# A two-layer graph transformer on one core: four buffers of gathered keys and values, an MLP in halves, and roots by a power

## The chip, the cores and the metric

The kernel runs on one core of one Trainium2 chip. The metric is the device time of one execution in microseconds. A core has a tensor engine (PE, with its weight loads listed apart as PEld), a vector engine (DVE), a scalar engine (ACT), GpSimd (POOL) and a sync engine (SP), each with its own queue of instructions, taken in order. DMA transfers are issued from SP, ACT and POOL; a gather or scatter by indices (DMA_INDIRECT) is issued from POOL.

## What is computed

3125 nodes of 256 features, 50000 edges, two layers. Layer 0 is a graph sum, a linear attention with MLP, and a dense mixture of eight experts. Layer 1, in which the change lies, adds an edge attention (`_L1_gnn_ref`), a "hyperbolic" branch (`_L1_mix_ref`) and a routed mixture of experts (`_L1_ffn_ref`, the two best of eight, plus a shared MLP). Shortened:

```python
# edge attention
q, k, v = feat @ Wq.T + bq, feat @ Wk.T + bk, feat @ Wv.T + bv          # 8 heads of 32
score = clip(einsum('ehd,ehd->eh', q[edge_dst], k[edge_src]) / sqrt(HD), -10, 10)
alpha = softmax of score over the edges of each edge_dst
wv = segment_sum(alpha * v[edge_src], edge_dst)
x = feat + wv @ Wp.T + bp
h = layernorm(x) * ln_g + ln_b
gnn = x + gelu(h @ W1.T + b1) @ W2.T + b2                                # 256 -> 1024 -> 256
# hyperbolic branch: norms, and a division by a norm, several times
n = clip(norm(u), 1e-15); tanh(n) * u / n; arctanh(min(n, 1 - 1e-5)) * p / n
# x = x + gnn + mix; then x = x + shared MLP + the two routed experts
```

Both branches take many reciprocal square roots of small vectors: one number a node for the layer norms and for the norms.

## The kernel before

*Tiles.* The nodes are 25 tiles of 125; `CHUNKS` are seven groups of four tiles (the last has one). The edges are sorted by target node; each node tile has a list of 17 x 128 edge slots, in three groups of 6, 6 and 5 (`GRP`): 75 groups in all.

*An order written by a planner.* Each stage is written as generators ("streams") that yield `Op(engine, cost, after, take, give)` before they issue instructions. `Flow.run` (L126) keeps a time for every engine and for every buffer, and at each step resumes the stream whose operation can start first; ties go to the lower urgency, the first argument of `flow.add`. `take` and `give` count buffers (`Flow(kvg=3, ...)`, L1478). When an operation is done its users may start after its end, its `lag`, and `HOP = 0.2` (L91, L143). The costs are figures in the code, in us; they decide the order of the instructions in each engine's queue and nothing else. The chip runs that order with semaphores.

*Layer 0* is recorded by a Flow of its own; its MLP uses the same `mlp_stream` (L636) with the name "m". *Layer 1* (`layer1`, L1443) is one Flow with these streams:

- `group` (L1498), one for each of the 75 groups: POOL gathers the keys and values of its 6 x 128 edges from `kvtab` into a buffer `kvg` (one DMA_INDIRECT for 128 edges, L1504); SP loads the tile's queries `q3`, the transposed one-hot matrix `ST` and the one-hot matrix `Sb`; PE spreads the queries over the edges (`qe`, L1540); DVE multiplies them into the keys (L1544), sums over a head (`sco`, L1563) and clips (L1568); ACT takes the exponential (L1570); DVE multiplies it into the values (L1573); PE sums the edges of each node (`es`, L1581), which gives the buffer `kvg` back.
- `attend` (L1585), one a tile: the division by the sum, a transpose `wvT`, the matmul `wp`.
- `mlp_stream` with the name "g", one a chunk of up to four tiles: layer norm on DVE with `rsqrt`, two transposes into PSUM, ACT's scaling into `hT`, eight pairs of matmuls `hp_g` (L683; 500 columns), a GELU each into one of eight buffers `hid` (L675), then the second product `dn_g` tile by tile (L697).
- `hyper` (L1612), one a tile, in pairs of tiles: SP loads `z`, ACT applies six ReLUs (L1625), PE transposes and multiplies into `cat` (L1642, L1644), a root `nn` a pair; then reciprocals and products on DVE, a transpose `oT` and the matmul `ft`. `hyper_end` (L1714), one a chunk: roots `n3` and `n4`.
- Then `route_in` (layer norm and logits), `routing`, `scatter`, and the experts: `shared` (L1968, matmuls `hp_s` and `dn_s`), `fetched` and `routed` (32 tiles of 256 rows, `rh` L2059 and `ry` L2074), `finish`, `collect`.

*A root* (`rsqrt`, L287) is a bit-level first guess by two integer operations and three Newton steps of three operations: eleven DVE instructions on a tile of one to four columns.

GELU and the exponential need different function tables on ACT; the compiler puts an ACT_TABLE_LOAD wherever the queue goes from one to the other.

Of the kernel before, what the change touches and what calls it, by code (L numbers as in the profile page):

```python
# [18 lines left out]
C = 256  # L19
E = 50000  # L20
P = 125
# [65 lines left out]
class Flow:  # L87
# [3 lines left out]
    HOP = 0.2  # L91
    TABLE = 1.28

    def __init__(self, **buffers):
        self.free = {}
        self.buffers = {tag: [0.0] * n for tag, n in buffers.items()}
        self.streams = []
        self.table = None
# [27 lines left out]
    def run(self):  # L126
        live = [s for s in sorted(self.streams, key=lambda s: s[:2]) if self._resume(s, None)]
        while live:
            best, at_ = None, None
            for s in live:  # L130
                t = self._start(s[3])
                if t is not None and (best is None or t < at_ - 1e-6):
                    best, at_ = s, t
            assert best is not None, "streams that wait for each other"
            op = best[3]
            for tag in op.take:
                self.buffers[tag].remove(min(self.buffers[tag]))
            end = at_ + op.cost
            self.free[op.eng] = end
            if op.table is not None:  # L140
                self.table = op.table
            done = Mark()
            done.time = end + op.lag + self.HOP  # L143
            for tag in op.give:
                self.buffers[tag].append(done.time)
            if not self._resume(best, done):
                live.remove(best)
# [3 lines left out]
def kernel(ctx: ExitStack, tc: tile.TileContext, a: dict, out: bass.AP):  # L151
# [71 lines left out]
    def row(pool, name, parts=P):  # L223
# [43 lines left out]
                   allow_small_or_imprecise_dtypes=True)  # L267
    tiny = keep.tile([128, 1], F32, name="tiny")
# [18 lines left out]
    def rsqrt(v, n, name, parts=P):  # L287

        y = small.tile([parts, n], F32, tag=f"rsy{n}", name=f"rsy_{name}", bufs=6)
        g = small.tile([parts, n], F32, tag=f"rsg{n}", name=f"rsg_{name}", bufs=6)  # L290
# [7 lines left out]
        return y  # L298

# [336 lines left out]
    def mlp_stream(c, inputs, name, pool_of, w1, w2, g, b, b1, done, start=None):  # L636

        t0, nt = CHUNKS[c]
        n = nt * P
        mv = small.tile([P, 4, 2], F32, tag=f"mv_{name}", name=f"mv_{name}{c}", bufs=2)  # L640
        for j in range(nt):
            m = yield Op("DVE", 0.6, [inputs[t0 + j]])
            st = small.tile([P, 6], F32, tag="st", name=f"st_{name}{c}_{j}")
            nc.vector.bn_stats(st, XN[c][:, j, :])
            nc.vector.bn_aggr(mv[:, j, :], st)
            m2 = yield Op("DVE", 0.42, [m])
            nc.vector.tensor_tensor(X[c][:, j, :], X[c][:, j, :], XN[c][:, j, :], OP.add)
        m = yield Op("DVE", 2.1, [m])
        var = small.tile([P, 4], F32, tag="rs", name=f"var_{name}{c}")
        nc.vector.tensor_scalar(var[:, :nt], mv[:, :nt, 1], 1e-5, None, op0=OP.add)  # L650
        rs = rsqrt(var[:, :nt], nt, f"{name}{c}")
        for j in range(nt):
            m = yield Op("DVE", 0.36, [m, m2])
            nc.vector.tensor_scalar(XN[c][:, j, :], XN[c][:, j, :], mv[:, j, 0:1],
# [3 lines left out]
        pt = [mm_tile([128, 512], f"tr_{name}_{c}_{k}") for k in range(2)]  # L658
        for k in range(2):
            for j in range(nt):  # L660
                nc.tensor.transpose(pt[k][:, j * P : (j + 1) * P],
                                    XN[c][:, j, k * 128 : (k + 1) * 128], ident[:P, :P])
        for k in range(2):
            m = yield Op("ACT", 0.56, [mk], take=["hT"] if k == 0 else [], give=["mm"])
            if k == 0:
                hT = pool_of().tile([128, 2, 4 * P], F32, tag="hT", name=f"hT_{name}_{c}")
# [3 lines left out]
        def gelu():  # L670
# [3 lines left out]
            hm = pool_of().tile([128, 4 * P], F32, tag="hid", name=f"hid_{name}{c}_{q}", bufs=8)  # L674
# [3 lines left out]
        for h in range(8):  # L678
            mk = yield Op("PE", 0.0035 * n, [m], take=["mm", "hid"],
                          give=["hT", "mlp"] if h == 7 else [])  # L680
            ps = mm_tile([128, 512], f"hp_{name}{c}_{h}")
# [6 lines left out]
        for j in range(nt):  # L688
            for q in range(0, 8, 4):
# [4 lines left out]
                if q == 0:  # L694
                    po = nm_tile([P, C], f"dn_{name}{c}_{j}")
# [4 lines left out]
            nc.vector.tensor_tensor(X[c][:, j, :], po, X[c][:, j, :], OP.add)  # L700
# [742 lines left out]
    def layer1(lists):  # L1443
# [23 lines left out]
        for m in range(6):  # L1467
# [10 lines left out]
        flow = Flow(kvg=3, S=3, Sb=2, ST=2, q3=2, qe=2, ed=1, mm=2, nm=3, z=1, cat=2, r=2,  # L1478
                    oT=1, ft=5, ch=2, sc=1, mlp=1, hT=1, hid=8,
                    mh=8, rhid=8, rw=2, xr=2, xrT=2, yr=2, to=3)  # L1480
        attended_ = [Mark() for _ in range(T)]
        mlp_, hyp_ = [Mark() for _ in CHUNKS], [Mark() for _ in CHUNKS]
# [15 lines left out]
        def group(b, gi, blk):  # L1498
# [3 lines left out]
            kvg = ep.tile([128, 6, 2 * C + NH], F32, tag="kvg", name=f"kvg_{nm}", bufs=3)  # L1502
# [82 lines left out]
        def attend(b, blk):  # L1585
# [15 lines left out]
            wT = ep.tile([128, 2, P], F32, tag="wT", name=f"wvT_{b}", bufs=2)  # L1601
# [10 lines left out]
        def hyper(t, pair, ch):  # L1612
# [6 lines left out]
            if t == t0:  # L1619
# [3 lines left out]
                for i in range(6):  # L1623
                    mk = yield Op("ACT", 0.43, [m])
# [7 lines left out]
            for i in range(4):  # L1632
                s, h = divmod(i, 2)
                last = i == 3 and t == t0 + nt - 1
                mk = yield Op("PE", 0.75 if s == 0 else 1.4, [pair["ready"]],
# [32 lines left out]
            if t == t0 + nt - 1:  # L1668
                m = yield Op("DVE", 2.3, [m, full])
# [3 lines left out]
                y = rsqrt(nn, nt, f"nn{t}")  # L1673
# [22 lines left out]
            m = yield Op("PE", 0.96, [m], take=["mm"], give=["r"])  # L1696
# [17 lines left out]
        def hyper_end(c, ch):  # L1714
            t0, nt = CHUNKS[c]
            m = yield Op("DVE", 2.3, ch["done"])
            n3, s3, n4 = ch["n3"][:, :nt], ch["s3"][:, :nt], ch["n4"][:, :nt]
            nc.vector.tensor_scalar(n3, n3, MIN_NORM ** 2, None, op0=OP.max)
            y = rsqrt(n3, nt, f"n3{c}")
# [12 lines left out]
            m = yield Op("DVE", 2.3, [m])  # L1732
            nc.vector.tensor_scalar(n4, n4, MIN_NORM ** 2, None, op0=OP.max)
            y = rsqrt(n4, nt, f"n4{c}")
# [44 lines left out]
        def after_all():  # L1779
            m = yield Op("SP", 0.5, mlp_ + hyp_)  # L1780
# [4 lines left out]
        def route_in(c):  # L1785
            t0, nt = CHUNKS[c]
            n = nt * P
            m = yield Op("DVE", 0.6 * nt + 2.1, [mlp_[c], hyp_[c], moe_])
# [179 lines left out]
        def shared(c):  # L1968
# [11 lines left out]
            for h in range(8):  # L1980
                tag = ("mm", "qe")[h % 2]
                mk = yield Op("PE", 0.0035 * n, [turned_[c], moe_], take=[tag, "mh"])
# [7 lines left out]
            for j in range(nt):  # L1990
                for q in range(0, 8, 4):
                    if j == 0 and q == 4:
                        yield from gelu()
                    m = yield Op("PE", 1.75, [acts[q + 3]], take=["nm"] if q == 0 else [],
                                 give=["mh"] * 8 if j == nt - 1 and q == 4 else [])
# [123 lines left out]
        for c, (t0, nt) in enumerate(CHUNKS):  # L2119
            flow.add(t0 + 8, mlp_stream(c, attended_, "g", lambda: lp, w1, w2, "gnn_g", "gnn_b", "gnn_b1",  # L2120
                                   mlp_[c], big_))
# [197 lines left out]
```

## Time and profile before

| | us |
|---|---|
| median of 3 runs | 2899.23 (2895.84 to 2901.83) |
| the profiled execution | 2883.45, its span 2881.6 |
| PE busy (instructions) | 2537.6, 88% (11409) |
| PE weight loads | 1836.7, 64% |
| DVE | 1390.3, 48% (3497) |
| ACT | 968.3, 34% (2001) |
| POOL | 1149.4, 40% (1145) |
| mean granted clock of PE | 0.946 |

Times in the profile are microseconds, unless they stand as ns. A line of the costliest groups reads: line of the kernel, engine, operation, output<-inputs, shapes, count | busy us, mean ns of one | idle us of the engine just before them, and what ended most of it. A line of waits reads: who waited at which line <- for whom: us in all, times, the longest. The page's row of slices gives the busy share in 40 equal parts of the span (72 us each) in tenths. Layer 0 fills about the first 18 slices, the attention of layer 1 the next eleven or so (the first gather of `kvg` starts at 1308.81 us), routing and experts the rest.

### The profile page before, as it was taken

The page shows a single profiled execution, that of the slowest core. Times are in us where ns is not written, and L with a number is a line of the kernel's source. Part 1 is how long each engine was busy: PE and PEld are TensorE (multiplying, and loading weights), DVE is VectorE, ACT ScalarE, POOL GpSimd, SP SyncE. Part 2 cuts the span into 40 slices and gives each one's busy share as a digit, 9 for nine tenths or more (in the row PEclk, how much of TensorE's full clock was granted, in tenths as well). Part 3 has the DMA queues.
Part 4 walks back from the last instruction along what each step waited for, and adds up shares of the span by engine and source line. Part 5 has one row for each costly group of instructions (what it writes and reads, how often), then busy time and mean ns, then how long its engine had stood idle before and what let it go on. Part 6 is the DMA issues. An engine that isn't in the chain of part 4 may idle for free. (4 is left out here: it accounts for less than half of the span.)

```text
span 2881.6 us, 32246 instructions
## 1 busy us (share of the span) xinstructions
PE 2537.6 (88%) x11409; PEld 1836.7 (64%) x11409; DVE 1390.3 (48%) x3497; ACT 968.3 (34%) x2001; POOL 1149.4 (40%) x1145
## 2 busy tenths in 40 slices
PE   3889988888998999996677888878888999999998
PEld 2556665655665555564556666666666668888886
DVE  5365123252443242456778798878798301111113
ACT  3673111122222343344334454434433212222221
POOL 3002667766673010004555554545441452222220
PEclk8979999999999999997889999999999999999999
DMA  4425555565562004317666665556550145555554
GB/s 106 134 95 174 153 172 169 158 182 162 158 197 84 25 26 125 82 37 243 187 183 201 189 192 171 173 170 185 166 156 17 41 142 189 196 192 192 192 174 139
DMA packets 186999, 427.01 MB, mean 148 GB/s; under 512 B 31434, under 2 KB 116554, under 8 KB 178635
## 3 DMA queue, kind: packets, MB, share of 16 engines
q0 software_dynamic: 80688, 281.78, 32.5%
q1 hardware_dynamic: 103593, 140.99, 15.7%
q10 hardware_dynamic: 2545, 2.09, 0.3%
q8 instruction: 92, 1.51, 0.2%
q14 instruction: 81, 0.66, 0.1%
HBM read 358.95 MB, written 65.74 MB: 147 GB/s over the span
## 5 line engine op out<-in xcount | busy, mean ns | idle before, releaser
L1504 POOL DMA_INDIRECT kvg<-kvtab,el x425 | 453.4, 1067 | 372.3 <-issue 111.3
L1063 POOL DMA_INDIRECT msg<-hs,el x425 | 421.9, 993 | 407.9 <-DMA hot<-S 209.6
L1175 ACT ACTIVATE fh<-fp,bnh,bns 128x500 f32<-128x500 f32 (+1 forms) x224 | 159.7, 723 | 411.1 <-PE fp L1171 288.9
L1581 PE MATMUL es<-kvg,S 128*125 128x264 f32 x850 | 231.9, 427 | 53.3 <-DVE kvg L1573 48.1
L1540 PE MATMUL qe<-q,ST 125*128 125x256 bf16 x1275 | 176.8, 280 | 74.2 <-DVE kvg L1544 53.9
L1186 DVE SCALAR_TENSOR_TENSOR x<-fy,f_w,x 125x256 f32<-125x256 f32 x200 | 95.8, 482 | 300.7 <-PE fy L1183 192.4
L2059 PE MATMUL rh<-xrT,rw 128*128 128x256 f32 x1024 | 237.3, 380 | 0.0
L1581 PEld LDWEIGHTS es<-kvg,S 128*125 128x125 f32 x850 | 170.5, 206 | 102.8 <-DVE kvg L1573 59.6
L1183 PE MATMUL fy<-f_Wo,fh 128*125 128x256 f32 x800 | 210.4, 386 | 29.1 <-DVE x L1186 18.6
L2047 ACT ACTIVATE rhid<-rh,rw 128x256 f32<-128x256 f32 x256 | 121.5, 475 | 337.1 <-PE rh L2059 312.8
L2074 PE MATMUL ry<-rw,rhid 128*128 128x256 f32 x1024 | 231.5, 379 | 0.0
L1092 PEld LDWEIGHTS <-S 128*125 128x125 bf16 x1275 | 158.8, 143 | 90.9 <-issue 72.4
L2074 PEld LDWEIGHTS ry<-rw,rhid 128*128 128x128 f32 x1024 | 194.6, 190 | 26.9 <-issue 0.5
L1092 PE MATMUL es<-msg,S 128*125 128x256 bf16 x1275 | 188.2, 284 | 22.3 <-DMA msg<-hs,el 13.0
L2059 PEld LDWEIGHTS rh<-xrT,rw 128*128 128x128 f32 x1024 | 189.4, 190 | 28.6 <-ACT rhid L2047 5.0
L2081 DVE TENSOR_TENSOR yr<-ry,rw 128x256 f32<-128x256 f32 x64 | 27.2, 425 | 357.6 <-PE ry L2074 357.6
L1540 PEld LDWEIGHTS <-ST 125*128 125x128 bf16 x1275 | 127.3, 100 | 113.6 <-issue 77.7
L1183 PEld LDWEIGHTS fy<-f_Wo,fh 128*125 128x125 f32 x800 | 143.1, 190 | 88.5 <-issue 40.1
L1171 PE MATMUL fp<-fh,f_W 128*128 128x500 f32 (+1 forms) x448 | 187.6, 545 | 4.2 <-ACT fh L1175 3.8
L1171 PE MATMUL fp<-xT_f,f_W 128*128 128x500 f32 (+1 forms) x448 | 188.5, 547 | 0.0
L1544 DVE TENSOR_TENSOR kvg<-qe,kvg 128x512 f32<-128x512 f32 (+1 forms) x225 | 143.1, 652 | 50.2 <-PE qe L1540 22.8
L1299 POOL TENSOR_TENSOR xn<-xn,row_bp 125x1024 f32<-125x1024 f32 (+1 forms) x7 | 13.8, 1974 | 379.4 <-DVE hx L1273 192.5
(422 smaller groups left out, 4242.3 us busy)
## 6 DMA issues: line engine op xcount, KB each, us to landing
db<-dlT SPq DMA_DIRECT2D x25, 544.0 KB
ST<-dlT SPq DMA_DIRECT2D x25, 544.0 KB
hot<-S SPq DMA_DIRECT2D x50, 187.5 KB
Sb<-hot SPq DMA_DIRECT2D x50, 187.5 KB
ztab<-z SPq DMA_DIRECT2D x18, 500.0 KB
z<-ztab SPq DMA_DIRECT2D x12, 750.0 KB
xs<-pad SPq DMA_DIRECT2D x1, 8224.0 KB
xr<-xs SPq DMA_DIRECT2D x32, 257.0 KB
```

Of the source, the lines that this page charges most:

```text
L1063: nc.gpsimd.indirect_dma_start(out=msg[:, i, :], out_offset=None, in_=hs3_rows, in_offset=bass.IndirectOffsetOnAxis(ap=el[:, b, g0 + i : g ...
L1092: nc.tensor.matmul(blk["po"], S[:, i, :], msg[:, i, r * C : (r + 1) * C], start=(g0 + i == 0 and r == 0), stop=(g0 + i == LE - 1 and r == 2))
L1171: nc.tensor.matmul(ps[q][:, :n], self.ws[e][i][:, k, q * 128 : (q + 1) * 128], h[:, k, :n], start=(k == 0), stop=(k == 1))
L1175: nc.scalar.activation(nxt[:, q, :n], ps[q][:, :n], AF.Relu, bias=self.sh[i][:, 2 * e + q : 2 * e + q + 1], scale=self.sc[i][:, 2 * e + q ...
L1183: nc.tensor.matmul(po, nxt[:, k, j * P : (j + 1) * P], self.ws[e][2][:, k, :], start=(k == 0), stop=(k == 1))
L1504: nc.gpsimd.indirect_dma_start(out=kvg[:, i, : 2 * C], out_offset=None, in_=kvtab, in_offset=bass.IndirectOffsetOnAxis(ap=el[:, b, g0 + i ...
L1540: nc.tensor.matmul(pq[i0][:, i, :], ST[:P, g0 + i0 + i, :], blk["q3"][:, r, :], start=(r == 0), stop=(r == 2))
L1544: nc.vector.tensor_tensor(kvg[:, i0 : i0 + k, :C], pq[i0][:, :k, :], kvg[:, i0 : i0 + k, :C], OP.mult)
L1581: nc.tensor.matmul(blk["pa"], S[:, i, :], kvg[:, i, C:], start=(g0 + i == 0), stop=(g0 + i == LE - 1))
L2047: nc.scalar.activation(hid[-1][:, q % 2, :], ps, AF.Gelu, bias=w1[:, 8 * C + q : 8 * C + q + 1])
L2059: nc.tensor.matmul(ps, w1[:, k * 4 * C + h * 128 : k * 4 * C + (h + 1) * 128], xrT[:, k, :], start=(k == 0), stop=(k == 1))
L2074: nc.tensor.matmul(po, hid[k // 2][:, k % 2, r * 128 : (r + 1) * 128], w2[:, k * C : (k + 1) * C], start=(k == 0), stop=(k == 7))
```

## The change

Six edits:

1. `kvg` has four buffers instead of three (in the planner and in the pool).
2. `mlp_stream` takes a part of a chunk: in layer 1 two tiles at a time, thirteen streams instead of seven, with `hT` and `hid` half as wide and the urgency `t0 + h_ + 6` instead of `t0 + 8`. `wT` has one buffer instead of two; the buffers of wide roots go from six to one.
3. Layer 1's planner counts 0.5 us instead of 0.2 from an operation to its users (`hop`).
4. A new `rsqrt_by_power` takes the layer norm's root in the MLP of layer 1 and the roots `nn`, `n3` and `n4`: one power on POOL, then one Newton step of three operations on DVE. The roots in layer 0 and in `route_in` stay.
5. Some of the planner's costs are others: z 0.55 for 0.43, cat 0.48 and 0.86 for 0.75 and 1.4, oT 0.62 for 0.96; the first product of the MLP 0.0039 a column for 0.0035, in both layers.
6. The shared MLP of the experts takes a token `shared`, so that the planner lets one chunk of it run at a time.

```diff
-    HOP = 0.2
-    def __init__(self, **buffers):
+    def __init__(self, hop=0.2, **buffers):
+        self.hop = hop
...
-            done.time = end + op.lag + self.HOP
+            done.time = end + op.lag + self.hop
...
+    minus_half = keep.tile([128, 4], F32, name="minus_half")
+    nc.vector.memset(minus_half, -0.5)
...
+    def rsqrt_by_power(v, n, name, m):
+
+        y = small.tile([P, n], F32, tag=f"rpy{n}", name=f"rpy_{name}", bufs=8)
+        g = small.tile([P, n], F32, tag=f"rpg{n}", name=f"rpg_{name}", bufs=8)
+        m = yield Op("POOL", 0.65, [m])
+        nc.gpsimd.tensor_tensor(y, v, minus_half[:P, :n], OP.pow)
+        m = yield Op("DVE", 0.5, [m])
+        nc.vector.scalar_tensor_tensor(g, y, -0.5, v, op0=OP.mult, op1=OP.mult)
+        nc.vector.tensor_tensor(g, g, y, OP.mult)
+        nc.vector.scalar_tensor_tensor(y, g, 1.5, y, op0=OP.add, op1=OP.mult)
+        return y, m
...
-    def mlp_stream(c, inputs, name, pool_of, w1, w2, g, b, b1, done, start=None):
+    def mlp_stream(c, inputs, name, pool_of, w1, w2, g, b, b1, done, start=None, part_=(0, 4)):
-        t0, nt = CHUNKS[c]
+        j0, cap = part_
+        t0, nt = CHUNKS[c][0] + j0, min(cap, CHUNKS[c][1] - j0)
...
+            m = yield Op("DVE", 0.17, [m])
+            var = small.tile([P, 4], F32, tag="mvar", name=f"var_{name}{t0}", bufs=len(CHUNKS))
+            nc.vector.tensor_scalar(var[:, :nt], mv[:, :nt, 1], 1e-5, None, op0=OP.add)
+            rs, m = yield from rsqrt_by_power(var[:, :nt], nt, f"{name}{t0}", m)
...
-                hT = pool_of().tile([128, 2, 4 * P], F32, tag="hT", name=f"hT_{name}_{c}")
+                hT = pool_of().tile([128, 2, cap * P], F32, tag="hT", name=f"hT_{name}_{t0}")
...
-            hm = pool_of().tile([128, 4 * P], F32, tag="hid", name=f"hid_{name}{c}_{q}", bufs=8)
+            hm = pool_of().tile([128, cap * P], F32, tag="hid", name=f"hid_{name}{t0}_{q}", bufs=8)
...
-        flow = Flow(kvg=3, S=3, Sb=2, ST=2, q3=2, qe=2, ed=1, mm=2, nm=3, z=1, cat=2, r=2,
+        flow = Flow(hop=0.5, kvg=4, S=3, Sb=2, ST=2, q3=2, qe=2, ed=1, mm=2, nm=3, z=1, cat=2, r=2,
...
-            kvg = ep.tile([128, 6, 2 * C + NH], F32, tag="kvg", name=f"kvg_{nm}", bufs=3)
+            kvg = ep.tile([128, 6, 2 * C + NH], F32, tag="kvg", name=f"kvg_{nm}", bufs=4)
...
-            wT = ep.tile([128, 2, P], F32, tag="wT", name=f"wvT_{b}", bufs=2)
+            wT = ep.tile([128, 2, P], F32, tag="wT", name=f"wvT_{b}", bufs=1)
...
-                m = yield Op("DVE", 2.3, [m, full])
+                m = yield Op("DVE", 0.4, [m, full])
...
-                y = rsqrt(nn, nt, f"nn{t}")
+                y, m = yield from rsqrt_by_power(nn, nt, f"nn{t}", m)
+                m = yield Op("DVE", 0.17, [m])
...
-                mk = yield Op("PE", 0.0035 * n, [turned_[c], moe_], take=[tag, "mh"])
+                mk = yield Op("PE", 0.0035 * n, [turned_[c], moe_],
+                              take=[tag, "mh"] + (["shared"] if h == 0 else []))
...
-            flow.add(t0 + 8, mlp_stream(c, attended_, "g", lambda: lp, w1, w2, "gnn_g", "gnn_b", "gnn_b1",
-                                   mlp_[c], big_))
+            for h_ in range(0, nt, 2):
+                flow.add(t0 + h_ + 6, mlp_stream(c, attended_, "g", lambda: lp, w1, w2, "gnn_g", "gnn_b",
+                                            "gnn_b1", mlp_[c][h_ // 2], big_, (h_, 2)))
```

## The prediction

> **What bounds the kernel now.** I began with the page's forty slices: where is the tensor engine (PE) full, and where not?
>
> ```profile
> PE   3889988888998999996677888878888999999998
> DVE  5365123252443242456778798878798301111113
> PEclk8979999999999999997889999999999999999999
> ```
>
> From slice 33 on (2375 us) PE is full and DVE nearly idle: the routed MLP costs what PE costs. In slices 18 to 29 both stand at 6 to 9 and neither is full. That is the attention of the second layer, which the change edits. I cut it out by windows (length, then busy us of PE, weight loads, DVE, ACT, POOL; then granted clock, DMA share, GB/s).
>
> ```profile
> 1308.00:2175.00 867.00, 688.44 (x3567) 528.13 (x3567) 698.31 (x1358) 362.28 (x894) 453.39 (x425) 0.91 0.60 183
> 1308.00:1525.00 217.00, 145.87 (x770) 114.52 (x770) 158.46 (x280) 78.22 (x214) 123.08 (x115) 0.84 0.69 210
> 1525.00:2175.00 650.00, 542.57 (x2799) 413.62 (x2798) 539.85 (x1079) 284.06 (x681) 330.31 (x311) 0.93 0.58 174
> 2350.00:2375.00 25.00, 19.85 (x76) 14.08 (x75) 2.04 (x5) 6.00 (x12) 0.95 (x1) 0.93 0.58 212
> ```
>
> Of 867 us PE is busy 79% and DVE 81%: two queues that wait for each other in turn. The waits of this stage say on what (total us, times, longest):
>
> ```profile
> POOL kvg L1504 <- PE qe L1540: 104.7, 20, 18.3
> PE qe L1540 <- DVE kvg L1544: 53.9, 31, 9.2
> PE es L1581 <- DVE kvg L1573: 48.1, 35, 6.1
> DVE kvg L1573 <- ACT kvg L1570: 12.6, 8, 5.5
> ```
>
> POOL's gathers wait for a buffer to come back; PE waits 102 us for the two products of a group on DVE. The chain of waits in this window gives its largest PE lines (es 7.1%, dn_g 5.2%, hp_g 4.6%, qe 4.0%) 20.9% and its largest DVE lines (4.9, 3.8, 3.5, 2.5%) 14.7%. So where work leaves DVE, I let 14.7/35.6 = 0.41 of it reach the end, and 0.59 where it is added to PE. That is a choice: the bounds are 0 and 1.
>
> **The change, part by part.** Counts and places come from the instruction order of both built programs, durations from the trace of before.
>
> *Roots.* A root is eleven DVE instructions in a row:
>
> ```profile
> 1343.19 0.17 DVE L291 TENSOR_SCALAR rsg_nn<-nn 125x2 int32<-125x2 int32 x1
> 1343.40 0.17 DVE L292 TENSOR_SCALAR rsy_nn<-rsg_nn 125x2 int32<-125x2 int32 x1
> ...
> 1345.36 0.17 DVE L1674 TENSOR_SCALAR s<-rsy_nn 125x2 f32<-125x2 f32 x1
> ```
>
> That is (1345.36 - 1343.19)/11 = 0.197 us each. The 27 roots of the hyperbolic branch (13 + 7 + 7) keep three on DVE: 27 x 8 x 0.197 = 42.6 us. The MLP's go from 7 x 12 instructions (with the epsilon) to 13 x 4: 32 x 0.197 = 6.3 us. DVE loses 49 us; times 0.41: **-20** (bounds 0 and -49).
>
> Each of the 40 roots now goes to POOL and back. The power is not in the trace; its nearest rows are the smallest two-operand operation and a one-column one:
>
> ```profile
> L1299 POOL TENSOR_TENSOR xn<-xn,row_bp 125x256 f32<-125x256 f32 x1 | 0.7, 745 | 27.6 <-PE qe L1540 27.6
> L805 POOL TENSOR_SCALAR pad<-part 128x1 f32<-128x1 f32 x1 | 0.2, 217 | 0.1
> L1504 POOL DMA_INDIRECT kvg<-kvtab,el x425 | 453.4, 1067 | 372.3 <-issue 111.3 <-PE qe L1540 104.7 <-DVE sco L1568 39.7
> ```
>
> 0.22 to 0.75 us; with two to four columns nearer the lower row, but with an operation not shown, so I take 0.6. The queue it joins weighs more. Gathers hold POOL (453.4 + 111.3)/867 = 65% of the stage, in groups of six, 6 x 1.33 = 8 us. DVE is in order: all behind a waiting root waits too, the products of later groups first, and then PE for those. In the new order 24 roots have over 5 us of other DVE work between the question and the use of the answer; that work hides them. Sixteen have 0 to 4.8 us, 1.9 on average. Such a root meets a group with chance 0.65 and waits half of it: 0.65 x 4 + 0.6 - 1.9 = 1.3 us, 16 x 1.3 = 21 us on DVE, x 0.41: **+8** (bounds 0, all at once; and 16 x (8 + 0.75 - 1.9) = 110).
>
> *Fourth buffer and larger distance.* One edit for the clock: a gather may run ahead by one more group, and the order puts more between an operation and its user. Bounds: 0, and the 102 us in which PE waits for the group's products. A buffer now returns every fourth group instead of every third, so a quarter of these waits: **-25**. Below nothing it is possible as well: SP's queue is moved too. In the new order the first q3 and ST loads stand behind the last five ztab stores, and some z loads one or two Sb loads later; z is what six ReLUs and PE's cat matmuls wait for. At 1312.75 the first z load was issued in before; two loads ahead of it cost about **+2** at the start.
>
> *MLP by two tiles.* PE makes 384 passes of 250 columns for 192 of 500 (32 of 125 stay).
>
> ```profile
> L2059 PE MATMUL rh<-xrT,rw 128*128 128x256 f32 x1024 | 237.3, 380 | 0.0
> L1985 PE MATMUL hp_s<-xT_f,pw1s 128*128 128x500 f32 (+1 forms) x224 | 88.8, 547 | 1.0 <-ACT xT_f L1804 1.0
> L675 ACT ACTIVATE hid_g<-hp_g,pv 128x500 f32<-128x500 f32 (+1 forms) x56 | 35.1, 633 | 33.5 <-PE hp_g L683 23.1 <-issue 7.7 <-PE qe L1540 2.4
> L675 ACT ACT_TABLE_LOAD x15 | 19.2, 1283 | 0.3
> ```
>
> At 256 columns a pass takes 237.3/1024 = 0.232 us, so 0.226 at 250; at 500 the passes stand 0.42 apart (weight loads at 2824.10 and 2824.52 in the timeline). 384 x 0.226 - 192 x 0.42 = 6.1 us (0 if exactly half; 19 at the stage's es rate, 231.9/850 x 250/264 = 0.258). Times 0.59: **+4**. ACT gets 104 GELUs of about 0.475 (the row of rhid) for 56 of 0.633, +14, and 26 scalings for 14, +5. It is idle 58% of the stage; that hides both. The tables are another thing: between the first and the last exponential the order holds 29 table loads before and 55 after, since GELU and exponential alternate more finely. A load takes 1.28 us and the next activation begins at once (a load at 1660.38, its exponential at 1661.67). 26 x 1.29 = 34 us more on ACT, 13 of the loads ahead of an exponential, on the path sco, exp, kvg. DVE waits 12.6 us there now for 75 groups. I take 13 x 1.29 = 17, a third of it felt: **+5** (bounds 0 and 34).
>
> The Trainium skill, "ScalarE: Activation LUTs", section "What ACT_TABLE_LOAD costs", speaks against this: a switch costs 1283 ns plus a drain of about 1380. The trace has the first and no second. By the page the 26 would cost 69 us and the sum would be about 5 us worse. "GPSIMD Engine Reference", section 4.1, sends elementwise work on tiles to VectorE; for a tile of four columns behind gathers the rows above decide.
>
> *Elsewhere.* In the first layer the planner books more for the MLP's first product, and its matmuls slide by a few places against the edges' (0, bounds +-5: PE is 85 to 95% busy there). Behind the routing PE idles 5.15 us in 2350 to 2375, until xr is read back; the new order lets three hidden blocks of the shared MLP run there (three times 1.7 us): **-4**.
>
> Sum: -20 + 8 - 25 + 2 + 4 + 5 - 4 = **-30 us**. The profiled execution took 2883.45 (span 2881.6), 16 below the median of the runs, 2899.2; by the median this gives **2869 us**.
>
> **The rivals.** (1) *Eaten up*: all 26 loads felt (+29 on my sum: 2898), or the fourth buffer brings nothing because POOL's waits put down to PE qe are the product's late return, which more distance doesn't shorten (+25: 2894). For it: 104.7 us name a qe matmul, which frees no buffer. Against it: POOL does wait 372.3 - 111.3 = 261 us at this line. (2) *Slower*: the root behind a group of gathers takes the place of the eleven instructions. Sixteen short covers, and a loop: a gather waits for the es matmul of four groups back, the root behind it for the gather, DVE for the root. It decides once all 40 roots cost DVE 94 us (38/0.41), 2.35 each; at 3.5 each: (140 - 94) x 0.41 = +19, 2918 us. Against it: 24 roots have cover. (3) *More*: both engines reach the later part's 83.5% from the start. PE's 694 us at 0.835 make 831 of 867, and DVE's work would allow less; with the -4 behind the routing, 2859 or below.
>
> **How the numbers follow.** Forecast together with (3) 0.58, its own range 2835 to 2890; (1) 0.20, between 2890 and 2905; (2) 0.22. A measurement here can tell about 0.2% (6 us) from no change. Of (1) half is still faster by that, 0.08 within, 0.02 slower: faster 0.68, same 0.08, slower 0.24. The range leaves one in ten on each side: 2826 to 2920.
>
> **What would show it.** Right: DVE's busy time 40 us or more lower, PE's waits L1544 and L1573 together well below 102, the stage from first gather to last es 25 to 35 us shorter, the MoE part the same to 5 us. Wrong: DVE idle before the first instruction after a power, put down to POOL, over 90 us in all; ACT's exponentials waiting for nothing but table loads while DVE waits for them; PE over 19 us busier in hp_g.

## The result, and the profile after

| | us |
|---|---|
| changed kernel, median of 4 runs | 2928.97 (2910.76 to 2937.72) |
| kernel before, median of 4 runs | 2897.53 (2893.91 to 2901.83) |
| ratio, 95% interval | 1.0103, 1.0056 to 1.0150 |
| profiled execution, changed (before) | 2910.76, span 2908.5 (2883.45, span 2881.6) |
| DVE busy | 1347.3 (1390.3) |
| ACT busy | 1013.6 (968.3) |
| POOL busy | 1167.8 (1149.4) |
| mean granted clock of PE | 0.941 (0.946) |

The change made the kernel 31 us slower; 2869 was forecast, and 2826 to 2920 as the range. The 2% verdict calls this the same; the interval does not.

The three rows of the forty slices that opened the prediction, of the changed kernel (72.7 us a slice):

```profile
PE   3888978989899999995788778887788999999998
DVE  5364122253534253354788677777778201111113
PEclk8989999999999999996899889998998999999999
```

DVE's 8s and 9s in slices 23 to 29 became 7s: the roots did leave it. PE did not fill up in exchange.

Where the 27 us between the two spans came in is read from windows cut at four instructions: first gather of `kvg`, first `es`, last `es`, first `hp_s` (the shared MLP), end. Columns: window, length, then busy us of PE, weight loads, DVE, ACT, POOL, then granted clock, DMA share, GB/s. The kernel before:

```profile
1308.80:1342.30 33.50, 16.54 (x90) 13.54 (x89) 11.51 (x27) 16.69 (x46) 16.25 (x17) 0.70 0.73 238
1342.30:2161.10 818.80, 658.12 (x3412) 504.02 (x3413) 676.73 (x1289) 337.92 (x829) 437.14 (x408) 0.92 0.60 183
2161.10:2224.70 63.60, 53.50 (x242) 40.05 (x241) 55.43 (x222) 19.50 (x46) 9.55 (x4) 0.92 0.06 19
2224.70:2881.60 656.90, 643.85 (x2922) 528.02 (x2922) 111.41 (x294) 164.32 (x326) 195.15 (x231) 0.99 0.48 160
```

The changed kernel, cut at the same instructions:

```profile
1312.70:1363.70 51.00, 20.19 (x96) 15.02 (x94) 16.56 (x34) 19.67 (x51) 22.73 (x24) 0.63 0.77 254
1363.70:2180.30 816.60, 659.32 (x3576) 537.56 (x3577) 626.86 (x1050) 377.35 (x890) 449.35 (x435) 0.91 0.58 178
2180.30:2250.10 69.80, 55.57 (x263) 47.38 (x261) 61.51 (x216) 23.12 (x64) 19.89 (x12) 0.85 0.06 18
2250.10:2908.50 658.40, 643.92 (x2922) 531.72 (x2922) 105.32 (x282) 163.58 (x326) 189.94 (x229) 0.99 0.48 159
```

First gather 3.9 us later, 17.5 more to the first `es`, 2.2 less in the middle, 6.2 more in the tail, 1.5 more in the experts: together the 26.9. The loss is at the start; the puzzle is the middle, where DVE has 50 us less to do and only 2 us were won.

The waits of the attention stage of the changed kernel (who waited at which line <- for whom: us, times, longest). L1526 is the gather, L1562 `qe`, L1566 and L1595 the two products, L1603 `es`, L307 the power:

```profile
POOL kvg L1526 <- PE es L1603: 60.4, 12, 13.3
POOL kvg L1526 <- PE qe L1562: 58.6, 15, 12.3
PE qe L1562 <- DVE kvg L1566: 57.7, 26, 7.9
DVE kvg L1566 <- remote: 49.2, 13, 16.3
POOL rpy_nn L307 <- DVE nn L1694: 42.2, 4, 19.4
POOL rpy_g L307 <- DVE var_g L671: 34.5, 5, 16.6
POOL rpy_n L307 <- DVE n L1741: 28.7, 4, 12.6
ACT wvT L1624 <- remote: 24.3, 4, 6.9
...
PE es L1603 <- DVE kvg L1595: 20.1, 12, 5.7
```

PE's waits for the two products fell from 102.0 to 77.8, as far as this trace names them (how far, the experiments tell). Two kinds of wait have grown. POOL stands 105 us at a power, for an operand of DVE, in 13 times; for 48 us of them gathers still stand behind in its queue, 57 lie after the last gather. And DVE and ACT wait for "remote": the view finds no instruction of this core that released them. What such a wait looks like (timeline: start, length, instruction, idle time before it):

```profile
1557.69 0.22 ACT L1681 ACTIVATION_READ_ACCUMULATOR sq<-cat 125x1 f32 x1
1563.70 0.37 ACT L1624 COPY wvT<-wvT 128x250 f32<-128x250 f32 x1 [5.79 <-remote]
...
1557.54 0.38 PE L1621 MATMUL wvT<-ident,sums 125*128 125x125 f32 x2
1557.75 1.48 PE L1666 MATMUL cat<-wxt,z 128*125 128x128 f32 x12
1564.12 2.07 PE L1628 MATMUL wp<-wp,wvT 128*125 128x256 f32 x4 [4.90 <-ACT wvT L1624]
```

By its record the transpose that the copy reads ended at 1557.92; ACT began the copy 5.8 us later, and PE's next matmul began only after the copy.

### The profile page after: what moved, and what is told of

Its sections match the earlier page's. It is cut to its first block, busy times and chain, and to the rows that moved or that the text cites. A ratio compares the mean times of both kernels' runs of the same rounds, so it can differ in the third digit from the quotient of the medians.

```text
span 2908.5 us, 32547 instructions
## 1 busy us (share of the span) xinstructions
PE 2539.8 (87%) x11601; PEld 1881.1 (65%) x11601; DVE 1347.3 (46%) x3250; ACT 1013.6 (35%) x2087; POOL 1167.8 (40%) x1185
## 5 line engine op out<-in xcount | busy, mean ns | idle before, releaser
L1526 POOL DMA_INDIRECT kvg<-kvtab,el x425 | 442.3, 1041 | 309.7 <-issue 121.6
L1562 PE MATMUL qe<-q,ST 125*128 125x256 bf16 x1275 | 185.6, 289 | 82.4 <-DVE kvg L1566 57.7
L1603 PE MATMUL es<-kvg,S 128*125 128x264 f32 x850 | 219.4, 410 | 25.2 <-DVE kvg L1595 20.1
L1562 PEld LDWEIGHTS <-ST 125*128 125x128 bf16 x1275 | 131.0, 103 | 128.1 <-issue 91.6
L1603 PEld LDWEIGHTS es<-kvg,S 128*125 128x125 f32 x850 | 166.8, 201 | 62.4 <-DVE kvg L1595 24.2
L1566 DVE TENSOR_TENSOR kvg<-qe,kvg 128x512 f32<-128x512 f32 (+1 forms) x225 | 144.6, 653 | 117.8 <-remote 49.2
```

The source lines that it names most:

```text
L1526: nc.gpsimd.indirect_dma_start(out=kvg[:, i, : 2 * C], out_offset=None, in_=kvtab, in_offset=bass.IndirectOffsetOnAxis(ap=el[:, b, g0 + i ...
L1562: nc.tensor.matmul(pq[i0][:, i, :], ST[:P, g0 + i0 + i, :], blk["q3"][:, r, :], start=(r == 0), stop=(r == 2))
L1566: nc.vector.tensor_tensor(kvg[:, i0 : i0 + k, :C], pq[i0][:, :k, :], kvg[:, i0 : i0 + k, :C], OP.mult)
L1603: nc.tensor.matmul(blk["pa"], S[:, i, :], kvg[:, i, C:], start=(g0 + i == 0), stop=(g0 + i == LE - 1))
```

## The experiments

Eighteen runs in six groups; each group ran on one chip beside the kernel before. The chips were of two sorts, and this turned out to be half of the answer: on some the kernel before takes 2742 to 2744 us, on others 2894 to 2901, as on the chip of the result. So times are read as ratios to before, and two kernels are compared within one sort. One thing limits all of them: an edit to a cost, a buffer or a root gives the planner other times, so it writes another order of instructions for every engine. A run measures the edit together with that order. "Buffers" and "tiles" are those of `kvg` and of one MLP stream.

| run | the changed kernel with | before, us | ratio, 95% interval |
|---|---|---|---|
| e1 | small tiles moved | 2743.6 | 0.9916 (0.9897 to 0.9936) |
| e2 | roots on DVE | 2743.6 | 0.9822 (0.9804 to 0.9841) |
| e3 | distance 0.2 | 2743.6 | 1.0039 (1.0026 to 1.0053) |
| e4 | 3 buffers | 2743.6 | 0.9966 (0.9948 to 0.9985) |
| e5 | nothing altered | 2742.2 | 0.9924 (0.9911 to 0.9937) |
| e6 | (the kernel before) | 2742.2 | 1.0004 (0.9994 to 1.0014) |
| e7 | roots on DVE, idle powers on POOL | 2742.2 | 0.9929 (0.9916 to 0.9941) |
| e8 | e1 and e2 together | 2742.2 | 0.9826 (0.9813 to 0.9838) |
| e9 | nothing altered | 2894.1 | 1.0135 (1.0101 to 1.0170) |
| e10 | roots on DVE, old cost in layer 0 | 2894.1 | 1.0084 (1.0057 to 1.0112) |
| e11 | 3 buffers, 4 tiles | 2894.1 | 0.9962 (0.9940 to 0.9983) |
| e12 | roots on DVE, distance 0.2 | 2894.1 | 1.0238 (1.0213 to 1.0263) |
| e13 | 3 buffers | 2742.5 | 0.9963 (0.9948 to 0.9978) |
| e14 | 3 buffers, 4 tiles | 2742.5 | 0.9943 (0.9929 to 0.9957) |
| e15 | roots on DVE | 2742.5 | 0.9819 (0.9804 to 0.9834) |
| e16 | 3 buffers, 4 tiles, roots on DVE | 2742.5 | 0.9950 (0.9936 to 0.9964) |
| e17 | 3 buffers | 2896.3 | 1.0053 (1.0029 to 1.0076) |
| e18 | roots on DVE, old cost in layer 0 | 2900.8 | 1.0111 (1.0082 to 1.0141) |

**The start: e1.** In the kernel before, the first load of `ST` is issued at 1289.25 us, between layer 0's stores; in the changed one at 1316.92, behind all of them. The addresses of the built programs say why: with four buffers the pool of `kvg` begins at 151,904 instead of 163,360 bytes, below the end of the last tiles of layer 0 (155,204), and the loads of the first group now come after the first gather. The timeline of DVE in the changed kernel shows the price:

```profile
1317.04 0.17 DVE L1497 TENSOR_TENSOR bh<-pv,bh 128x6 f32<-128x6 f32 x1
1323.39 0.96 DVE L1544 TENSOR_SCALAR ST<-ST,part 128x2176 bf16<-128x2176 bf16 x1 [6.19 <-DMA ST<-dlT]
1325.97 0.69 DVE L1566 TENSOR_TENSOR kvg<-qe,kvg 128x512 f32<-128x512 f32 x1 [1.61 <-issue]
```

Before, `ST` was ready at 1295 and the first product ran at 1314.74. e1 gives the old order back by placing 3.7 KB of small tiles lower:

```diff
         ep = pool_("l1e", side="right")
+        eq = pool_("l1q", side="right")
...
-            sco = ep.tile([128, 6, NH], F32, tag="sco", name=f"sco_{nm}", bufs=3)
+            sco = eq.tile([128, 6, NH], F32, tag="sco", name=f"sco_{nm}", bufs=3)
```

(`sums` and `wT` likewise.)

> The changed kernel with one edit: the small tiles sco, sums and wT (3.7 KB a partition) get a pool of their own below the pool of kvg, so that the four kvg buffers begin above the last tiles of layer 0 again; the orders of q3_0 and ST_0 in SP's queue go back to where they were in the kernel before, ahead of the last ztab stores. Theory A (the room of the fourth buffer delays the start): the first es matmul comes at about 1343 us instead of 1363.7, the time falls by 15 to 21 us, to 2908 to 2914. Theory B (the start is lost later anyway, as the stage waits for something else): under 6 us, 2923 or more.

0.9916 against 0.9924 of the kernel unaltered (e5): nothing. From first gather to first `es` it took 42.0 us, e5 41.5. The first product did come at once (1239.05 us, 5.7 after the first gather), but the first `es` did not: the first exponentials (1273.28 us) stand in ACT's queue behind the ReLUs of the second load of `z` (issued 1261.93 us, the ReLUs start at 1268.95). The theory that placement loses the start fell on this sort of chip; on the other e1's edit wasn't tried. With three buffers the same stretch takes 38.1 and 39.7 us (e4, e13), so some 2 to 3 us of it are the fourth buffer's, and 6 to 8 us over the 32.0 of the kernel before (e6) stay without it. On the chips of the result's sort it is otherwise: the two profiles with three buffers (e11, e17), where `ST` is issued 20 us before the first gather again, take 39.4 and 39.3 us, the five with four buffers 50.5 to 52.6. So 11 to 13 us of the start go with the fourth buffer there; its place and its earlier gathers are not parted.

**The reference: e5, e6, e9.** The two kernels unaltered.

> The changed kernel itself, unaltered, on the chip of the other runs, as their reference. Times of different chips differ (the kernel before took 2897 us on the first and 2744 on that of e1 to e4), so single edits are read against this run. Theory A (the loss of about 1% is the kernel's): 1.005 to 1.015 of before. Theory B (part of the loss belonged to the first chip, whose engines stood still together for some us at a time): 0.995 to 1.004.

> The kernel before itself, for a profile on the same chip: ratio 1.000 to 0.2%. From the first es matmul to the first hp_s about 823 us, if layer 0 and the experts take what they take in e1 to e4; 16 to 20 us less from the first gather to the first es than the changed kernel, if the loss at the start is the kernel's.

> The changed kernel once more, for a ratio on one more chip. On the chip of the first result it took 1.010 of before, on that of e5 0.992. Theory A (the chip of the first result stalls: ACT, DVE and PE there stand 116, 64 and 45 us in the attention stage for nothing that the profile shows, against 7, 0 and 0 in e5): where before takes about 2742 us the ratio is 0.990 to 0.995; where before takes about 2897 us it is above 1. Theory B (the ratio varies freely from chip to chip): anything else.

The sign of the result depends on the chip: 0.9924 in e5, below what either of its theories had, and 1.0135 in e9, as its Theory A had it. The windows of e6 (before) and e5 (changed), cut as above. e6:

```profile
1222.40:1254.40 32.00, 14.76 (x91) 12.12 (x90) 11.75 (x27) 16.46 (x46) 16.27 (x17) 0.77 0.80 251
1254.40:2019.00 764.60, 640.56 (x3413) 493.04 (x3414) 675.21 (x1289) 336.77 (x829) 445.09 (x408) 0.95 0.63 196
2019.00:2082.70 63.70, 53.56 (x242) 40.13 (x240) 55.53 (x222) 19.50 (x46) 9.55 (x4) 0.92 0.06 19
2082.70:2739.10 656.40, 643.84 (x2922) 527.75 (x2922) 111.26 (x294) 164.02 (x326) 195.07 (x231) 0.99 0.48 160
```

e5:

```profile
1231.30:1272.80 41.50, 16.43 (x96) 12.42 (x94) 16.50 (x34) 19.32 (x51) 22.85 (x24) 0.66 0.93 313
1272.80:1999.60 726.80, 630.11 (x3576) 518.85 (x3577) 622.39 (x1050) 376.55 (x890) 468.43 (x435) 0.95 0.66 200
1999.60:2068.90 69.30, 54.94 (x262) 46.61 (x260) 61.03 (x215) 23.10 (x64) 19.90 (x12) 0.85 0.06 18
2068.90:2727.10 658.20, 643.70 (x2922) 531.68 (x2922) 105.88 (x283) 163.91 (x326) 190.22 (x229) 0.99 0.48 159
```

Here the middle shrank by 37.8 us; 8.9 us were lost before the first gather and 9.5 from there to the first `es` (16 to 20 had been expected), in the tail 5.6, in the experts 1.8. The experts take 656 to 663 us on any chip. What differs in the views are waits without a releaser ("issue": none found; "remote": none of this core). Adding up each engine's between first and last `es` (us):

| | PE | DVE | ACT | first to last es |
|---|---|---|---|---|
| before, chip of the result | 39 | 43 | 66 | 818.8 |
| changed, chip of the result | 45 | 64 | 116 | 816.6 |
| changed, e9 | 51 | 87 | 134 | 848.1 |
| 3 buffers, e17 | 48 | 58 | 84 | 829.8 |
| 3 buffers, 4 tiles, e11 | 34 | 54 | 102 | 805.5 |
| before, e6 | 0 | 0 | 6 | 764.6 |
| changed, e5 | 0 | 0 | 7 | 726.8 |
| 3 buffers, e13 | 1 | 0 | 6 | 743.5 |
| 3 buffers, 4 tiles, e14 | 0 | 0 | 22 | 742.4 |

On chips of the result's sort such waits of up to 12 us are frequent; on the other sort there are hardly any. I call the sorts stalling and quiet below. The middle of the changed kernel is 90 us longer in the profile of the result than in e5, and 121 in e9; that of the kernel before 54 us longer in the profile of the result than in e6.

The sums can't carry more than that, for two reasons that the traces show. First, the views find a releaser by the recorded updates of semaphores, and in the profiles of the stalling chips 15 to 17% of the updates that PE, DVE and ACT make are not recorded (in that of the result 7490 of 8957 are there), while on quiet chips none is missing. A wait for "issue" on a stalling chip can be one whose releaser is missing from the trace, and waits named by releaser, such as the 102.0 and 77.8 us of PE, are too small there. Second, the waits for "remote", 122 of the 224 us in the row of the changed kernel on the chip of the result, all end within 0.15 us of an update of PE's semaphore, 1.9 to 7.8 us after the last recorded end of a matmul that makes one. In the example above PE's last record ahead of the copy ends at 1559.23, and its updates come at 1560.11, 1561.54, 1562.26 and 1563.68, the last just before the copy. So ACT and DVE did not stop by themselves there: they waited for PE, which was later than its records say. Why it was late is open, and so is whether that is what takes the gain.

**The roots: e2, e15, e7, e8, e10, e18.** e2 (and e15, the same kernel) takes the root back to DVE:

```diff
-        m = yield Op("POOL", 0.65, [m])
-        nc.gpsimd.tensor_tensor(y, v, minus_half[:P, :n], OP.pow)
-        m = yield Op("DVE", 0.5, [m])
...
+        m = yield Op("DVE", 2.1, [m])
+        return rsqrt(v, n, name), m
```

e7 does so too, but issues the power on POOL besides, into a tile that nobody reads:

```diff
+        yield Op("POOL", 0.65, [m])
+        nc.gpsimd.tensor_tensor(p, src, minus_half[:P, :n], OP.pow)
+        m = yield Op("DVE", 2.1, [m])
+        return rsqrt(v, n, name), m
```

> The changed kernel with the 40 roots back on DVE as eleven instructions in a row. DVE's busy time goes up by about 43 us to 1390, POOL loses 40 powers. Theory A (the round trip through POOL's queue eats what DVE saves: 54 us of POOL waiting for a DVE operand in front of gathers): same or faster, 2905 to 2930. Theory B (the 49 us of DVE are worth 0.41 of their length, as predicted): 15 to 25 us slower, 2944 to 2954.

> e2's kernel again (the changed one with roots on DVE). Where before takes about 2742 us: 0.982 as in e2. Where it takes about 2894: about 1.007, as e10, since only layer 0's order parts the two.

> Roots on DVE as in e2, and besides each root the power on POOL at the same place of the planner, whose result nobody reads (for n4 of a copy): POOL still waits for a DVE operand 40 times with the gathers behind it, DVE never waits for POOL. Theory A (what hurts is the gathers that stand behind a power that waits for DVE): within 10 us of the changed kernel, at least 30 us above e2. Theory B (what hurts is DVE waiting for an answer from behind the gathers): within 10 us of e2. Theory C (the order that the planner writes around a root of 2.1 us in one piece is the better one): also within 10 us of e2; B and C part in e8 to follow.

> e1 and e2 together: small tiles below kvg, roots on DVE; four buffers, MLP halves, distance 0.5 stay. Theory A (start and roots are two separate losses): the gain of e1 over e5 on top of e2, about 2685 us where before has 2744. Theory B (the start's loss is made up later, since DVE and POOL have slack in the stage): equal to e2 within 5 us.

Eleven instructions on DVE beat one on POOL and three on DVE by 1.0% (0.9822 and 0.9819 against 0.9924, 28 us), the sign of e2's Theory A. Between 12 and 20 us of it come in the middle (726.8 to 706.8 and 714.8) and 18 to 19 in the tail (69.3 to 50.3 and 50.9). The tail is longer by work, not by waiting: DVE is busy 61.0 of its 69.3 us in e5 and 46.3 of 50.3 in e2, because more of the layer norms of `route_in` are left behind the last `es`; no wait of DVE for a power lies there. In e7 the powers answer nobody, and the ratio is that of the changed kernel, 0.9929: the powers alone cost about 28 us against e2, and what they take off DVE gives nothing on top. The waits of POOL and DVE, over the stage, in e5:

```profile
POOL rpy_g L307 <- DVE var_g L671: 30.8, 4, 16.6
POOL rpy_nn L307 <- DVE nn L1694: 23.5, 4, 9.3
POOL rpy_n L307 <- DVE n L1741: 21.3, 3, 11.2
...
DVE rpg_n L309 <- POOL rpy_n L307: 14.6, 8, 2.9
...
DVE rpg_nn L309 <- POOL rpy_nn L307: 7.7, 3, 7.3
...
DVE rpg_g L309 <- POOL rpy_g L307: 6.2, 3, 4.4
```

and in e7:

```profile
POOL rpy_nn L311 <- DVE nn L1695: 33.8, 5, 9.8
...
POOL rpy_g L311 <- DVE var_g L672: 25.0, 4, 10.5
...
POOL rpy_n L311 <- DVE n L1742: 16.0, 3, 11.5
...
POOL rpy_g L311 <- DVE sco L1591: 13.3, 1, 13.3
```

DVE waits 28.5 us for powers in e5 and not at all in e7; POOL waits 76 and 88 us at powers in the lines shown. So DVE's waiting (e7's Theory B) is not needed for the loss. That the gathers held behind a power make it (Theory A) is not shown either. Of all of POOL's waits for DVE at powers, 82 us in e5 and 105 in e7, 59 and 51 come after the last gather, with none behind. Between first and last `es` all engines together wait 5 us for a gather to land in e5, 6 in e7 and 10 in e2, and a group's first product begins a median of 10.0, 9.5 and 10.5 us after its last gather instruction has ended: the gathers are in time. Where e7 loses to e2, DVE waits longer for `qe` (31.9 us against 14.8) and for the load of `ST` (14.2 against 6.2). The queues of PE, DVE and ACT are in another order in e7 than in e2, so a held queue and a worse order are not parted. e8 adds e1's edit to e2: 0.9826, equal to e2, as its Theory B had it.

e10 and e18 are e2 with the old cost in layer 0:

```diff
-            mk = yield Op("PE", 0.0039 * n, [m], take=["mm", "hid"],
+            mk = yield Op("PE", (0.0035 if name == "m" else 0.0039) * n, [m], take=["mm", "hid"],
```

> e2 (roots on DVE) with the planner's old cost of the MLP's first product, 0.0035, in layer 0 alone; layer 1 is as in e2. The first gather of kvg started at 1230 to 1234 us in six kernels with 0.0039 out of seven and at 1222 us in the kernel before. Theory A (the new order of layer 0 costs what this shows): the first gather at about 1222 us, 5 to 10 us faster than e2, ratio 0.979 to 0.981. Theory B (layer 0 is bound by PE, the order doesn't matter, as predicted: 0, bounds 5 to either side): ratio 0.982 to 0.983.

> e10's kernel again. e10 met a stalling chip, where its first gather (1318.8 us) stood among those of the kernels with 0.0039 (1318.4 to 1322.4). Where before takes about 2742 us: Theory A (the new order of layer 0 costs what e5 to e6 show, 1231.3 against 1222.4): first gather at 1219 to 1225 us, 6 to 10 us below e2 and e15 (2695 to 2697), ratio 0.979 to 0.980, the fastest of all. Theory B (no cost): first gather at 1226 to 1238, ratio 0.982. Where before takes about 2894: 1.008 as e10, and the question stays open.

Both met stalling chips. Their first gathers (1318.8 and 1315.0 us) lie up to 7 us before those of e9, e11, e12 and e17 (1318.4 to 1322.4), but that of the result, with the new cost, came at 1312.7: whether layer 0's order costs anything is not settled. On these chips the roots on DVE, together with the old cost in layer 0, gain 0.5% at most (1.0084 and 1.0111 against 1.0135 and 1.0103).

**The distance: e3, e12.** The edit is `hop=0.2` for `hop=0.5`, in e12 on top of e2.

> The changed kernel with the planner's distance back at 0.2. Between the first and the last exponential ACT has 44 table loads instead of 54 (28 in the kernel before). Theory A (the larger distance only reorders, its worth is in PE's waits for DVE, which fell by 33 us): slower by 10 to 20 us, 2940 to 2950. Theory B (the larger distance costs by table loads and stalls of ACT): faster by 5 to 15 us, 2914 to 2924.

> e2 with the planner's distance back at 0.2. Theory A (the distance is worth about 31 us by itself, as e3 against e5 has it: 1.0039 against 0.9924): 25 to 35 us slower than e2, ratio 0.991 to 0.995. Theory B (the distance was worth so much only because the powers need a longer way): under 10 us slower than e2, ratio below 0.986.

Without the larger distance it is 1.0039 against 0.9924, 31 us slower: the middle grows by 53 us (779.7), the tail shrinks by 25 (44.4). In e12 against e10, on one chip, the loss is 1.5%, 45 us, with layer 0's cost as a second difference. Theory A had the sign in both, with too small a size: without the distance there is no gain, powers or not, four buffers or not. How the distance works was not found: PE's waits for the two products are the same with it and without (74.2 us in e5, 74.3 in e3).

**Buffers and halves: e4, e13, e17, e11, e14, e16.** Three buffers are `kvg=3` in the planner and `bufs=3` in the pool; four tiles:

```diff
-            for h_ in range(0, nt, 2):
-                flow.add(t0 + h_ + 6, mlp_stream(c, attended_, "g", lambda: lp, w1, w2, "gnn_g", "gnn_b",
-                                            "gnn_b1", mlp_[c][h_ // 2], big_, (h_, 2)))
+            for h_ in range(0, nt, 4):
+                flow.add(t0 + h_ + 8, mlp_stream(c, attended_, "g", lambda: lp, w1, w2, "gnn_g", "gnn_b",
+                                            "gnn_b1", mlp_[c][h_ // 4], big_, (h_, 4)))
```

> The changed kernel with three buffers of kvg, in the planner and in the pool; MLP halves, roots by power, distance 0.5 stay. The start is restored as in e1 because the pool is smaller. Theory A (the start costs about 18 us and the fourth buffer gives nothing later): about 2911, equal to e1 within 5 us. Theory B (the fourth buffer gives about the 25 us of the prediction in the rest of the stage): 15 to 25 us above e1, 2930 to 2937.

> e4's kernel (the changed one with three buffers) again; the ratio of before tells the sort of chip. Where before takes about 2742 us: 0.9966 as in e4. Where it takes about 2894 (the stalling sort, on which the changed kernel had 1.0135 and e11, with the MLP by four tiles besides, 0.9962): Theory A (there the halves cost, by more and shorter instructions): 1.010 to 1.014. Theory B (there the fourth buffer costs): 0.995 to 1.000.

> The changed kernel with three buffers once more (e4, e13: 0.9966 and 0.9963 on chips that do not stall). On a chip where before takes about 2894 us: Theory A (there the halves of the MLP turn the gain into a loss): 1.010 to 1.014, as the changed kernel (1.0135). Theory B (there the fourth buffer does it): 0.995 to 1.000, as e11 (0.9962). Where before takes about 2742: 0.9965, and the question stays open.

> e4 (three buffers, roots by power, distance 0.5) with the MLP by four tiles again: it tells what the halves alone are worth. Table loads between the first and the last exponential 40 instead of 46. Theory A (the halves cost what was predicted, 4 us of PE and 5 us of table loads): 5 to 12 us faster than e4, ratio 0.992 to 0.995. Theory B (the halves help by themselves, since a GELU of 250 columns lets exponentials through sooner): slower than e4 by 5 us or more, ratio above 0.998.

> e11's kernel again (three buffers, MLP by four tiles, roots by power, distance 0.5). Where before takes about 2894 us: 0.9962 as in e11. Where it takes about 2742: Theory A (the halves cost a little, as predicted, 9 us): 0.992 to 0.995 against 0.9966 of e4. Theory B (the halves gain where nothing stalls): above 0.999.

> Three buffers, MLP by four tiles, roots on DVE, distance 0.5: what is left of the change is the distance, the costs and the token. Theory A (powers cost about 1% on either sort of chip, as e2 against e5 and e10 against e9 have it between 0.5 and 1.0%): 0.5 to 1.0% below e14. Theory B (the powers hurt only beside four buffers, whose gathers crowd POOL's queue): equal to e14 within 0.2%.

On quiet chips the fourth buffer is worth 0.4% (0.9963 to 0.9966 without, 0.9924 with: 11 us) and the halves cost 0.2% (0.9963 against 0.9943: 5 us, close to the resolution; e14's Theory A). e4 lies 11 us above e1, between its two theories. On stalling chips the two together cost 1.7%, 50 us, measured on one chip (e9 against e11, 1.0135 against 0.9962). Between them stands e17 (1.0053): the halves 0.9%, the fourth buffer 0.8%. But e17 ran on another chip than e9 and e11, and the changed kernel itself differs by 0.3% between two stalling chips (1.0103, 1.0135). So neither theory of e17 held alone, and the shares are rough. e16 against e14 (0.9950, 0.9943): with three buffers and four tiles the powers cost nothing, e16's Theory B. Their 28 us need the fourth buffer or the halves; which, and whether by a fuller queue on POOL, was not tested.

The fastest kernel on quiet chips is the change with its roots left on DVE (0.982). On stalling chips it ran only with the old cost in layer 0, and is slower than before; there, of the kernels tried, only e11, three buffers and four tiles with the larger distance, stays below (0.9962), and it does so on both sorts (e14: 0.9943).

## Why the prediction was wrong, by its steps

- *The step that failed.* On the chip of the result it is the terms for the fourth buffer and the halves (-25, with the distance, and +4 +5) and for the start (+2). On chips of its sort the buffer and the halves together cost 50 us, 11 of them in the start (e9 against e11), and without the two the same change is 0.4% faster than before (e11). The start measured +21.4 us on the chip of the result (3.9 and 17.5). The middle, for which -20 +8 -25 +4 +5 = -28 had been added up, gave 2 us there; the tail lost 6.2 and the experts 1.5. Why the buffer and the halves cost in the middle there and not on quiet chips stays open. On quiet chips the terms that failed are the roots and the start.
- *What bounds the kernel.* "Two queues that wait for each other in turn" left a third thing out. The same trace held, between first and last `es`, 39 us of PE, 43 of DVE and 66 of ACT that waited for "issue" or "remote"; the chain from which the factor 0.41 was taken begins with "issue 10.3%", and the prediction had no term for it. On the chip of the result these sums grew to 45, 64 and 116, where they are absent the middle gave 38 us. That goes together in e5, e6 and e9; as the records are incomplete on the one sort, it doesn't show that such waits take the gain.
- *Roots, -20 +8.* DVE fell by 43.0 us (49 were counted). The sign of the whole was wrong: +28 on quiet chips instead of -12. The prediction priced DVE waiting behind a group of gathers; that wait was 7.6 us on the chip of the result, as far as it is recorded, and 28.5 in e5, where 21 were estimated. What it left out is what the powers cost without any answer, about 28 us (e7); by which way is open. A power took 0.72 to 1.09 us in the mean, 0.6 was taken:

```profile
L307 POOL TENSOR_TENSOR rpy_n<-n,minus_half 125x4 f32<-125x4 f32 (+1 forms) x14 | 15.2, 1086 | 35.4 <-DVE n L1741 28.7 <-DVE n L1757 5.2 <-DVE rpg_nn L309 1.2
L307 POOL TENSOR_TENSOR rpy_g<-var_g,minus_half 125x2 f32<-125x2 f32 (+1 forms) x13 | 10.0, 770 | 36.4 <-DVE var_g L671 34.5 <-PE cat L1664 1.8
L307 POOL TENSOR_TENSOR rpy_nn<-nn,minus_half 125x2 f32<-125x2 f32 (+1 forms) x13 | 9.4, 724 | 43.5 <-DVE nn L1694 42.2 <-issue 1.2
```

  Behind the bar stands POOL's idle time before the power: 115 us in all. The advice of the Trainium skill, "GPSIMD Engine Reference", section 4.1, to leave elementwise work to VectorE, which the prediction set aside for so small a tile, fits e2 and e15, and with three buffers and four tiles (e16) it makes no difference.
- *Buffer and distance, -25.* Sign right and size too small on quiet chips: 31 for the distance (e3) and 11 for the buffer (e4, e13), each taken out alone; on stalling chips the buffer costs. The mechanism was not the one named. Where the record is complete, PE's waits for the two products fell from 91.0 to 74.2 us, not by a quarter; before (e6), then changed (e5):

```profile
PE es L1581 <- DVE kvg L1573: 52.8, 49, 3.6
PE qe L1540 <- DVE kvg L1544: 38.2, 41, 5.2
...
PE qe L1562 <- DVE kvg L1566: 38.7, 26, 8.0
PE es L1603 <- DVE kvg L1595: 35.5, 27, 4.1
```

  And they are the same without the distance (e3), which is worth 31 us. POOL's waits at the gather fell from 310.4 to 217.2 us (e6, e5), and are 231.0 without the distance (e3) and 270.9 with three buffers (e13): they go more with the buffer than with the distance.
- *Start, +2.* 17.5 us from first gather to first `es` on the chip of the result, 9.5 between e6 and e5, and 3.9 and 8.9 before the first gather. The move of the loads was seen and booked at 2 us; that one of them, `ST`, holds DVE and PE was not followed to its end.
- *Halves and tables, +4 +5.* 5 us on quiet chips (e13, e14). `hp_g` went from 100.2 to 107.5 us, 6.1 were counted. On stalling chips they cost about 26 us, by two chips (e17, e11). The drain that the Trainium skill, "ScalarE: Activation LUTs", adds to a switch is not in this trace either; the exponential begins 0.01 us after its table:

```profile
1637.61 1.28 ACT L1592 ACT_TABLE_LOAD   x1
1638.90 0.24 ACT L1592 ACTIVATE kvg<-sco 128x48 f32<-128x48 f32 x1
```

- *Experts' boundary, -4.* Did not come: the experts took 1.5 us more, and PE's gap stands in 2375 to 2400 now (6.0 us idle). *Layer 0, 0 to 5 either way*: open.
- *The rivals.* "Slower" had the sign and 2918, but the wait it asked for, 94 us of DVE (38/0.41 is 93), did not come. On quiet chips the forecast's sign held: -19 us by the medians of e5 and before (2723.2, 2742.2), where -30 was forecast. That is luck: roots and start cost more than was added up, distance and buffer gave more.

## What to carry to other kernels

An instruction moved to an engine that issues gathers can cost more than its own time and the wait for its answer: forty powers that nobody reads cost about 28 us here (e7). A kernel that issues the instruction for nobody measures that cost, but where a planner writes the order, it measures the new order with it; to part the two, the order of the other queues has to be held. Before waits without a releaser are read as stops, count whether the trace has an update for every instruction that makes one. And before a per cent is forecast from one profile, take the ratio on more than one chip: the same change was 0.992 on one and 1.0135 on another.

## What the hardware did that was not expected

The same two kernels differ by 5 to 8% between chips (before 2742 and 2894 to 2901 us; changed 2723 and 2929 to 2941), nearly all of it ahead of the experts, which take 656 to 663 us everywhere. For the kernel before 86 of the 142 us between two profiles come ahead of the first gather of `kvg`, and 54 between first and last `es`. On the slower chips ACT and DVE wait for updates of PE's semaphore that come up to 8 us after PE's recorded work (in the profile of the result), and about a sixth of the updates is not recorded; on the faster ones neither occurs. Over the stage from first to last `es` of the changed kernel the granted clock is lower on the slower sort (0.91 against 0.95), and PE's busy time is longer (659 against 630 us). What makes the difference is open.
